# Attention and quantized feed-forward on one core: the values of a unit moved in front of the next scores, both in 64x64 tiles, with division and rotations moved to other places

## The chip, the cores and the metric

The kernel runs on one NeuronCore of a Trainium2 chip. The metric is the device time of one execution in microseconds (us); lower is better. A profile of one execution comes with it: it records every instruction of the engines and every transfer. The engines are TensorE (PE in the profile, with its weight loads as PEld), VectorE (DVE), ScalarE (ACT), GpSimd (POOL) and SyncE (SP), which here only starts transfers (DMAs).

## The reference

One transformer layer over 4 sequences of 512 tokens, 1024 channels, 16 heads of 64. Everything is float32 except the int8 weight of the second part.

```python
q = (x @ w_q.T).reshape(4, 512, 16, 64); k = ...; v = ...
q, k = rope(q), rope(k)                       # x * cos + rotate_every_two(x) * sin
scores = where(causal, einsum('bhqd,bhkd->bhqk', q, k), -1e9) / sqrt(64)
attn = softmax(scores, axis=-1)
out = einsum('bhqk,bhkd->bhqd', attn, v).reshape(4, 512, 1024)
x = layernorm(x + out @ w_out.T)
x = layernorm(x + x @ (weight * scales[:, None]).T)
```

## The kernel before

**Units.** A unit is one sequence and one pair of heads; there are 32 (`units`, L133), and the loop at L572 takes them one after the other. First come the units of sequences 0 and 1 in turn, then those of 2 and 3. While a unit `u` is in attention, TensorE also makes the q, k and v products of the units that follow: a product is 24 matmuls of 128x128 by 512 columns (`product`, L268: 16 of the parts h and l into one PSUM tile, 8 of the part d into another). These matmuls are dealt out as tickets by `take(n)`; a turn of the loop takes 72, in the order k of `u+1`, v of `u+1`, q of `u+2`. They fill the time in which TensorE would wait for the softmax.

**One turn of the loop** (L572 to L607): `scores(u)`: four blocks of 128 queries, in three groups (`GROUPS`, L121: blocks 0 and 1; block 2; block 3), each with its own PSUM tile; block `i` is multiplied with the keys of blocks 0 to `i`; the two heads sit in the two halves of the partitions, so a matmul has 64 rows and 128 columns of weights. `maxima` adds the causal mask to the diagonal block (VectorE, L427; for the three units in `BUSY` TensorE adds it, L419) and takes the maximum of each row (L430). `softmax` has ScalarE take the exponential with the sum of each row (L444), VectorE the reciprocal (L452) and GpSimd multiply the row by it (L458). `transposes` (L475) turns a group by 32x32 blocks on VectorE (L463), writes it to memory (`turned`, L464) and reads it back with keys on the partitions (`prT`, L472). `attend(u-1)` multiplies the transposed shares of the unit before with its values, 8 matmuls of 128 rows and 64 columns of weights, after 18 tickets (L490); ScalarE copies the result (L498) and starts its write to `ao` (L499).

**Other work in the turn.** At the 16th matmul of a product ScalarE takes the first sum out of PSUM into `tA` (L295), at the 24th VectorE joins the second sum to it (L318). For q and k, SP then starts two transfers that swap even and odd rows into `rot` (L249), and `rope` does two multiplications and an addition on VectorE (L235, L236, L242). The values are turned by `turn_values` (L463, L464, L482). After every second unit the weights change: `load_w` (L181) brings 512 KB for each of q, k, v into one of three stage buffers, ScalarE makes the part h and a scaled copy (L214, L215), VectorE the parts l and d (L219, L223). `later` and `run` put such steps into named slots of the turn.

**Order.** Between L502 and L608 TensorE, VectorE and ScalarE run in the order in which the program emits the work (`manual_schedule`). SP and GpSimd do not: the order of their instructions is left to the scheduler of the framework. After the loop come the output projection (L199), the first layer norm and the feed-forward part (L676).

Of the kernel before, what the change touches and what calls it, by code (L numbers as in the profile page):

```python
# [26 lines left out]
MASKED = -3.0e38  # L27
# [11 lines left out]
def attention_ffn_kernel(  # L39
# [29 lines left out]
    pdp = pds.enter_context(tc.tile_pool(name="pd", bufs=3, space=PSUM))  # L69

    ident = const.tile([P, P], FP, name="ident")
    mask, unit = (const.tile([P, P], BF, name=name) for name in ("mask", "unit"))
    cos_sb = const.tile([P, 2, S], FP, name="cos_sb")
    sin_sb = const.tile([P, 2, S], FP, name="sin_sb")
    eps_sb = const.tile([P, 1], FP, name="eps_sb")

# [3 lines left out]
    for n in (512, 384):  # L80
        nc.tensor.matmul(warm[:, :n], lhsT=sin_sb[:, 0, :P], rhs=sin_sb[:, 0, :n], start=True, stop=True)

    make_identity(nc, ident)
    make_identity(nc, unit)
    nc.gpsimd.memset(mask, 0.0)
    nc.gpsimd.affine_select(
        out=mask,
        in_=mask,
        pattern=[[-1, P]],
        compare_op=ALU.is_ge,  # L90
        fill=MASKED,
        base=0,
        channel_multiplier=1,
    )
    nc.gpsimd.memset(eps_sb, EPS)

# [31 lines left out]
    turned = {g: tc.dram_tile([R, P, w * 2 * Q], FP, name=f"turned_{g}") for g, w in enumerate(WIDE)}  # L128
    turned["v"] = tc.dram_tile([R, P, NI * Q], FP, name="turned_v")
# [99 lines left out]
    with tc.tile_pool(name="raw", bufs=2) as rawp, tc.tile_pool(name="qk", bufs=2) as qkp, ExitStack() as heads:  # L229
        def rope(u, k):  # L230

            raw, rot = prod.pop((u, k)), prod.pop(("rot", u, k))
            if u not in qk:
                qk[u] = qkp.tile([P, 2, S], FP, tag="qk", name=f"qk_{u}")
            nc.vector.tensor_mul(rot, rot, sin_sb[:, k, :])  # L235
            nc.vector.tensor_mul(raw, raw, cos_sb[:, k, :])  # L236
            out = qk[u][:, k, :]
            if k == 0:

                out = out.rearrange("p (i r s) -> p r i s", i=NI, r=R)  # L240
                raw, rot = (t.rearrange("p (r i s) -> p r i s", i=NI, r=R) for t in (raw, rot))
            nc.vector.tensor_add(out, raw, rot)  # L242

        def swap(u, k):

            raw = prod[u, k]
            rot = prod["rot", u, k] = rawp.tile([P, S], FP, tag="rot", name=f"rot_{u}_{k}", bufs=2)
            for p in range(2):
                nc.sync.dma_start(out=rot[p::2, :], in_=raw[1 - p :: 2, :])  # L249

        def raw_tile(u, k):
            tag = "v" if k == 2 else "raw"
            t = prod[u, k] = rawp.tile([P, S], FP, tag=tag, name=f"{tag}_{u}_{k}", bufs=1 if k == 2 else 2)
            return t
# [13 lines left out]
        def product(u, k, n):  # L268
# [24 lines left out]
            if n == 2 * NC - 1:  # L293
                prod["tA"] = rawp.tile([P, S], FP, tag="tA", name=f"tA_{u}_{k}")
                nc.scalar.activation(prod["tA"], ps, AF.Copy, scale=1.0 + X12)  # L295
                if x_next:
                    new_sequence(u, b_next, False)
                if more:
# [6 lines left out]
                    vector = ((u - 1, "first"), (u - 1, "late"), (u, "between"))[k]  # L305
                    if u == 1:
                        vector = (None, vector, (1, "between"))[k]
                    if last and k != 1:
# [5 lines left out]
                        later(*d, lambda: diff_w(k))  # L314
                    else:
                        later(*vector, lambda: split_w(k))
            if n == NT - 1:
                nc.vector.scalar_tensor_tensor(raw_tile(u, k), ps, -X12, prod["tA"], op0=MUL, op1=ADD)  # L318
                if k < 2:
                    swap(u, k)  # L320
                    slot = ("first" if last else "between" if u % 2 else "late") if k == 0 else "turn"
                    later(u - 1, slot, lambda: rope(u, k))
# [70 lines left out]
        probs, prT, stats, s_ps = {}, {}, {}, {}  # L393

        def scores(u):
            nmx = st1.tile([P, 2 * NI], FP, tag="nmx", name=f"nmx_{u}")
            den = st1.tile([P, 2 * NI], FP, tag="den", name=f"den_{u}")
            rden = st1.tile([P, 2 * NI], FP, tag="rden", name=f"rden_{u}")
            stats[u] = nmx, den, rden
            t = qk.pop(u)  # L400
            keys = t[:, 1, :].rearrange("p (r s) -> p r s", r=R)
            for g, blocks in enumerate(GROUPS):
                ps = pdp.tile([P, 2, 512], FP, tag="d", name=f"s_{u}_{g}")
                s_ps[u, g] = ps
                for i, at in blocks:
                    n = (i + 1) * P
                    for j in range(2):
                        rows = slice(j * D, (j + 1) * D)
                        nc.tensor.matmul(  # L409
                            ps[:, j, at : at + n],  # L410
                            lhsT=t[rows, 0, ts(i, P)],
                            rhs=keys[rows, :, : (i + 1) * Q],
                            start=True,
                            stop=u not in BUSY,
                        )
                    if u in BUSY:
                        diag = ps[:, :, at : at + n].rearrange("p a (r s) -> p a r s", r=R)[:, :, :, ts(i, Q)]
                        for j in range(2):
                            nc.tensor.matmul(diag[:, j], lhsT=unit, rhs=mask, start=False, stop=True)  # L419

        def maxima(u, g):
            nmx, den, rden = stats[u]
# [80 lines left out]
        with tc.manual_schedule(  # L503
# [68 lines left out]
            for u in range(NU):  # L572
                scores(u)
                run(u, "early")
                for g in range(3):
                    maxima(u, g)
# [195 lines left out]
```

## Time and profile before

| what | value |
|---|---|
| median of 3 runs | 1020.24 us (1019.99 to 1022.3) |
| span of the profiled execution | 1020.7 us |
| start up to the first scores | 33.4 us |
| the 32 units, from the first scores to the end of the last values | 33.4 to 738 us |
| output projection and feed-forward | 738 to 1020.7 us |
| TensorE busy between 381.1 and 681.3 us | 300.2 of 300.2 us |
| VectorE, ScalarE busy there | 257.0 us, 135.8 us |
| share of time the 16 DMA engines are busy there | 0.70 |
| one turn of the loop, in the plain stretches | 21.45 us |

In the profile an arrow reads "written from": `s<-qk` is the score tile made from the rotated q and k. A float32 matmul shows two records, one for each of two passes over its columns. An idle time before an instruction is put down to what ended it. Where the same turn of the loop is spoken of, its times are counted from a first matmul of that turn.

### The profile page before, as it was taken

The numbers are of one execution on the slowest core, as the hardware profiler recorded it, in microseconds if no ns is written. First come the engines' busy times: TensorE is split into PE (matmuls) and PEld (weight loads), VectorE is DVE, ScalarE is ACT, GpSimd is POOL, SyncE is SP. The second block draws the span as 40 slices with busy tenths as digits, with TensorE's granted clock in tenths as the row PEclk, the third lists the DMA queues.
The fourth block names the chain that finished last, engine by engine and source line by source line (L and its number), as shares of the span: only waits on it lengthen the run. The fifth ranks groups of instructions, "written<-read, shape, count | busy, mean of one in ns | idle before, by whom it ended". The sixth has DMA issues, their size and how long they took to land.

```text
span 1020.7 us, 13748 instructions
## 1 busy us (share of the span) xinstructions
PE 999.7 (98%) x4628; PEld 742.0 (73%) x4628; DVE 852.8 (84%) x1246; ACT 389.0 (38%) x841; POOL 201.1 (20%) x283
## 2 busy tenths in 40 slices
PE   9999999999999999999999999999899999999997
PEld 4667777777777667777777777776578888888885
DVE  5998888888888999788898888889877877878776
ACT  4534444354444435445344453445332122121110
POOL 0122332222322322332223322232100000000000
PEclk9999999999999999999999999999999999999999
DMA  7576676767768787576866758688635465564551
GB/s 288 170 233 220 203 234 190 263 195 223 232 193 261 250 254 227 183 253 192 253 210 206 247 173 273 217 250 278 223 108 160 124 160 143 128 168 104 145 103 62
DMA packets 264022, 204.09 MB, mean 200 GB/s; under 512 B 147600, under 2 KB 220304, under 8 KB 263824
## 3 DMA queue, kind: packets, MB, share of 16 engines
q1 hardware_dynamic: 256176, 184.60, 60.0%
q10 hardware_dynamic: 5616, 10.75, 2.9%
q0 software_dynamic: 2160, 7.87, 1.9%
q8 instruction: 37, 0.61, 0.3%
q14 instruction: 33, 0.27, 0.1%
HBM read 112.46 MB, written 73.92 MB: 183 GB/s over the span
## 4 chain that ended last, share of the span: by engine, by line
PE 85%; DMA 5%; issue 4%; DVE 4%; POOL 1%; SPq 0%; ACT 0%; DVEq 0%; POOLq 0%
PE p L276 43%; PE y L199 15%; PE f L676 11%; PE o L490 7%; PE s L409 6%; PE pw L261 2%; DMA turned<-pr 2%; DVE pr L463 1%; POOL pr L458 1%; DMA sx<-in_wo 1%; DMA prT<-turned 1%; DMA raw_x<-in_xT 1%; DVE w_l L219 1%; DMA va<-turned_v 0%; DMA turned_v<-v 0%
## 5 line engine op out<-in xcount | busy, mean ns | idle before, releaser
L458 POOL TENSOR_SCALAR pr<-pr,rden 128x128 f32<-128x128 f32 (+3 forms) x256 | 189.9, 760 | 525.9 <-DVE rden L452 414.5
L276 PE MATMUL p<-x_h,w_h 128*128 128x512 f32 x736 | 290.2, 394 | 0.0
L276 PE MATMUL p<-x_l,w_l 128*128 128x512 f32 x736 | 286.8, 390 | 0.0
L276 PE MATMUL p<-x_d,w_d 128*128 128x512 f32 x736 | 190.9, 395 | 3.1 <-DVE v L318 2.5
L276 PEld LDWEIGHTS p<-x_h,w_h 128*128 128x128 f32 x736 | 138.1, 188 | 50.3 <-issue 22.0
L444 ACT ACTIVATE pr<-s,nmx 128x128 f32<-128x128 f32 (+3 forms) x256 | 131.5, 531 | 112.6 <-DVE nmx L430 107.1
L276 PEld LDWEIGHTS p<-x_d,w_d 128*128 128x128 f32 x736 | 135.5, 188 | 36.4 <-issue 5.1
L276 PEld LDWEIGHTS p<-x_l,w_l 128*128 128x128 f32 x736 | 138.2, 188 | 28.1
L295 ACT ACTIVATE tA<-p 128x512 f32<-128x512 f32 x92 | 55.2, 600 | 218.4 <-PE p L276 218.4
L463 DVE STREAM_TRANSPOSE pr<-pr 128x768 f32<-128x768 f32 (+1 forms) x96 | 99.7, 1057 | 24.4 <-POOL pr L458 23.7
L430 DVE TENSOR_REDUCE nmx<-s 128x2 f32<-128x256 f32 (+3 forms) x128 | 101.9, 820 | 3.0
L199 PE MATMUL y<-x_l,w_l 128*128 128x512 f32 x256 | 100.1, 391 | 2.1 <-DVE w_l L219 2.1
L199 PE MATMUL y<-x_h,w_h 128*128 128x512 f32 x256 | 100.4, 392 | 0.5 <-DVE row L208 0.5
L676 PE MATMUL f<-wf,x1lo 128*128 128x512 f32 x240 | 93.6, 390 | 1.1 <-DVE x1lo L650 1.1
L676 PE MATMUL f<-wf,x1hi 128*128 128x512 f32 x240 | 93.5, 389 | 0.0
L409 PE MATMUL s<-qk 64*128 64x384 f32 (+3 forms) x512 | 80.2, 446 | 1.0 <-DVE qk L242 1.0
L490 PE MATMUL o<-prT,va 128*64 128x256 f32 (+3 forms) x512 | 77.7, 446 | 2.2 <-DMA prT<-turned 1.7
L223 DVE TENSOR_TENSOR w_d<-w_h,w_l 128x1024 fp32r<-128x1024 f32 x60 | 74.0, 1233 | 1.5
L318 DVE SCALAR_TENSOR_TENSOR raw<-p,tA 128x512 f32<-128x512 f32 x61 | 41.8, 686 | 37.1 <-PE p L276 37.0
L490 PEld LDWEIGHTS o<-prT,va 128*64 128x64 f32 x512 | 34.8, 138 | 48.6 <-issue 42.6
L199 PE MATMUL y<-x_d,w_d 128*128 128x512 f32 x256 | 64.9, 393 | 1.6 <-DVE x_d L177 1.2
L409 PEld LDWEIGHTS s<-qk 64*128 64x128 f32 x512 | 41.4, 186 | 22.4 <-issue 11.3
(112 smaller groups left out, 1162.1 us busy)
## 6 DMA issues: line engine op xcount, KB each, us to landing
turned<-pr SPq DMA_DIRECT2D x64, 384.0 KB, 3.4
rot<-raw SPq DMA_DIRECT2D x128, 128.0 KB, 2.8
turned<-pr SPq DMA_DIRECT2D x32, 512.0 KB, 4.5
prT<-turned SPq DMA_DIRECT2D x32, 512.0 KB, 5.2
prT<-turned SPq DMA_DIRECT2D x32, 384.0 KB, 3.9
turned_v<-v SPq DMA_DIRECT2D x32, 256.0 KB, 5.0
va<-turned_v SPq DMA_DIRECT2D x128, 64.0 KB, 2.6
prT<-turned SPq DMA_DIRECT2D x32, 256.0 KB, 3.3
```

Of the source, the lines that this page charges most:

```text
L199: nc.tensor.matmul(ps, lhsT=r[part][:, c, :], rhs=w[part][:, c, :], start=n in (0, 2 * NC), stop=n in (2 * NC - 1, NT - 1),)
L223: nc.vector.tensor_tensor(d, h, l, SUB)
L276: nc.tensor.matmul(ps, lhsT=w[part][:, c, :], rhs=r[part][:, c, :], start=n in (0, 2 * NC), stop=n in (2 * NC - 1, NT - 1),)
L295: nc.scalar.activation(prod["tA"], ps, AF.Copy, scale=1.0 + X12)
L318: nc.vector.scalar_tensor_tensor(raw_tile(u, k), ps, -X12, prod["tA"], op0=MUL, op1=ADD)
L409: nc.tensor.matmul(ps[:, j, at : at + n], lhsT=t[rows, 0, ts(i, P)], rhs=keys[rows, :, : (i + 1) * Q], start=True, stop=u not in BUSY,)
L430: nc.vector.tensor_reduce(nmx[:, 2 * i : 2 * i + 2], ps[:, :, at : at + n], AX.X, ALU.max, negate=True)
L444: nc.scalar.activation(pr[:, :, at // P : at // P + i + 1, j, :], ps[:, j, at : at + n].rearrange("p (r k s) -> p r k s", r=R, s=Q), AF.Ex ...
L458: nc.gpsimd.tensor_scalar(p, p, rden[:, m : m + 1], 1.0, ALU.mult, ALU.mult)
L463: nc.vector.transpose(t, t)
L490: nc.tensor.matmul(ps[j * D : (j + 1) * D, kb * P :], lhsT=v[:, kb, 2 * j : 2 * j + 2, :].rearrange("p a s -> p (a s)"), rhs=t[:, :, 4 * k ...
L676: nc.tensor.matmul(ps, lhsT=part[:, c, :], rhs=wfv[:, c, o], start=(c == 0 and part is hi), stop=(c == NC - 1 and part is lo),)
```

## The change

Part by part:

1. **Place and tiling of the matmuls.** `attend(u-1)` stands right in front of `scores(u)`. Both work in tiles of 64 rows by 64 columns of weights. The halves of odd blocks are swapped in the order of tokens (`by_row`), and keys that lie after all queries of a half block are left out. The values of the upper and the lower 64 keys of a block go to two PSUM banks; ScalarE copies one and VectorE the other, GpSimd adds them. The PSUM tile of the values is now that of score group 0 (`ps_d[0]`).
2. **Division.** The shares are no longer divided (no L458). The sums of the rows are inverted, turned, written to memory and fetched again spread over the partitions (`shares`, `fetch_shares`), and GpSimd multiplies the values by them (`attended`).
3. **Rotations** of all units but the first run on GpSimd.
4. **Order.** Largest block first: groups 2, 1, 0. The reading back of the turned shares (`fetch`) stands apart from the writing and after the next 8 tickets. GpSimd and SP now also run in the order of the program, and the write to `ao` is started by SP.
5. The masks are built otherwise, with 32 small transfers at the start; `tA` is gone (the first sum goes straight into the raw tile); raw tiles have one buffer each; some slots of `later` are others.

```diff
-    pdp = pds.enter_context(tc.tile_pool(name="pd", bufs=3, space=PSUM))
+    pdp = pds.enter_context(tc.tile_pool(name="pd", bufs=1, space=PSUM))
+    ps_d = [pdp.tile([P, 2, 512], FP, name=f"s_{g}") for g in range(3)]
...
+        def rope(u, k, engine=nc.gpsimd):
+            pair = prod.pop((u, k))
+            raw, rot = pair[:, 0, :], pair[:, 1, :]
...
-            nc.vector.tensor_mul(rot, rot, sin_sb[:, k, :])
-            nc.vector.tensor_mul(raw, raw, cos_sb[:, k, :])
-            nc.vector.tensor_add(out, raw, rot)
+            engine.tensor_tensor(rot, rot, sin_sb[:, k, :], MUL)
+            engine.tensor_tensor(raw, raw, cos_sb[:, k, :], MUL)
+            engine.tensor_tensor(qk[u][:, k, :], raw, rot, ADD)
...
-                    vector = ((u - 1, "first"), (u - 1, "late"), (u, "between"))[k]
+                    vector = ((u - 1, "first"), (u - 1, "late"), (u - 1, "last"))[k]
...
+                    elif k < 2:
+                        later(*vector, lambda: split_w(k))
                     else:
-                        later(*vector, lambda: split_w(k))
+                        later(*vector, lambda: low_w(k))
+                        later(u, "then", lambda: diff_w(k))
...
-                    slot = ("first" if last else "between" if u % 2 else "late") if k == 0 else "turn"
-                    later(u - 1, slot, lambda: rope(u, k))
+                    later(u - 1, "turned_q" if k == 0 else "turned_k", lambda: rope(u, k))
...
@@ scores @@
+            for g in (2, 1, 0):
+                blocks = GROUPS[g]
+                ps = s_ps[u, g] = ps_d[g]
                 for i, at in blocks:
+                    for c in range(2):
+                        early = i * P + c * D
+                        if i % 2 != c:
+                            pieces = ((0, (i + 1) * P),)
+                        elif c == 0:
+                            pieces = ((0, early + D),)
+                        else:
+                            pieces = ((0, i * P), (early, early + D))
+                        for j in range(2):
+                            rows = slice(j * D, (j + 1) * D)
+                            for s0, s1 in pieces:
+                                nc.tensor.matmul(
+                                    ps[c * D : (c + 1) * D, j, at + s0 : at + s1],
+                                    lhsT=t[rows, 0, early : early + D],
+                                    rhs=t[rows, 1, s0:s1],
...
@@ softmax @@
-                    nc.gpsimd.tensor_scalar(p, p, rden[:, m : m + 1], 1.0, ALU.mult, ALU.mult)
...
+        def shares(u):
+            nmx, den = stats.pop(u)
+            nc.vector.reciprocal(rden[:, : 2 * NI], den)
+            t = st1.tile([P, Q], FP, tag="rdenT", name=f"rdenT_{u}")
+            nc.vector.transpose(t, rden)
+            nc.sync.dma_start(out=turned["d"].rearrange("a c s -> (a c) s"), in_=t)
+
+        def fetch_shares(u):
+            share[u] = otp.tile([P, R, P], FP, tag="share", name=f"share_{u}")
+            for j in range(2):
+                nc.sync.dma_start(
+                    out=share[u][j * D : (j + 1) * D],
+                    in_=turned["d"][:, j * NI : (j + 1) * NI, :].rearrange("a c s -> a (c s)").partition_broadcast(D),
+                )
...
@@ attend @@
+            for kb in range(NI):
+                for h in range(2):
+                    for j in range(2):
+                        rows = slice(h * D, (h + 1) * D)
...
+                        if h == kb % 2:
+                            piece(kb * P, later_blocks(kb))
+                        else:
+                            c = 1 - kb % 2
+                            piece(kb * P + c * D, t[rows, 2 * c : 2 * c + 2, 4 * kb, j, :])
+                            if kb < NI - 1:
+                                piece((kb + 1) * P, later_blocks(kb + 1))
+            nc.scalar.copy(o[0], ps[:, 0, :])
+            nc.vector.tensor_copy(o[1][:, D:], ps[:, 1, D:])
+
+        def attended(u):
+            nc.gpsimd.tensor_tensor(o[:, D:], o[:, D:], o1[:, D:], ADD)
+            o_by = o.rearrange("p (i a s) -> p i a s", i=NI, s=Q)
+            nc.gpsimd.tensor_tensor(o_by, o_by, share.pop(u).rearrange("p a (i s) -> p i a s", s=Q), MUL)
+            nc.sync.dma_start(out=ao[b][:, hp, :], in_=o)
...
@@ the turn of the loop @@
+                if u:
+                    attend(u - 1)
                 scores(u)
                 run(u, "early")
+                for g in (2, 1):
+                    maxima(u, g)
+                    softmax(u, g)
+                fetch_values(u)
+                if u:
+                    attended(u - 1)
+                run(u, "turned_q")
+                take(18)
+                transposes(u, 2)
+                maxima(u, 0)
+                softmax(u, 0)
+                transposes(u, 1)
+                transposes(u, 0)
                 run(u, "between")
                 run(u, "then")
+                take(8)
+                shares(u)
+                for g in (2, 1, 0):
+                    fetch(u, g)
+                fetch_shares(u)
                 run(u, "after")
                 run(u, "first")
                 run(u, "turn")
                 run(u, "mid")
+                take(10)
                 run(u, "second")
                 take(12)
+                run(u, "turned_k")
                 run(u, "late")
                 take(12)
                 if u + 1 < NU:
                     turn_values(u + 1)
+                run(u, "last")
                 take(12)
                 run(u, "end")
```

## The prediction

> **What bounds the kernel now.** I read the page's busy shares first, then the chain of waits in order of time, then single engines over one turn of the loop, then the transfers.
>
> ```profile
> PE 999.7 (98%) x4628; PEld 742.0 (73%) x4628; DVE 852.8 (84%) x1246; ACT 389.0 (38%) x841; POOL 201.1 (20%) x283
> ...
> 466.92 2.36 PE s L409 x16
> 469.28 4.32 PE p L276 x18
> 473.60 2.31 PE o L490 x16
> 475.91 12.46 PE p L276 x54
> 488.37 2.36 PE s L409 x16
> ...
> L409 PE MATMUL s<-qk 64*128 64x512 f32 x128 | 33.1, 594 | 0.0
> L261 PE MATMUL pw<-raw_x,raw_w 128*128 128x512 f32 x48 | 21.7, 606 | 0.3 <-DMA raw_x<-in_xT 0.3
> ...
> 482.82 0.60 SPq L181 DMA_DIRECT2D sw<-in_wq  x1
> 508.54 1.05 ACT L214 ACTIVATE w_h<-sw 128x1024 fp32r<-128x1024 f32 x1
> 524.63 0.58 SPq L181 DMA_DIRECT2D sw<-in_wq  x1
> 527.25 1.84 SPq L472 DMA_DIRECT2D prT<-turned  x2
> ...
> 466.85:509.75 42.90, 42.90 (x210) 31.44 (x209) 36.47 (x54) 19.28 (x47) 11.60 (x16) 1.00 0.70 221
> ...
> prT<-turned SPq DMA_DIRECT2D x32, 512.0 KB, 5.2
> ao<-ot ACTq DMA_DIRECT2D x32, 256.0 KB, 2.1
> sw<-in_wq SPq DMA_DIRECT2D x14, 512.0 KB, 5.7
> ```
>
> The chain is TensorE alone: scores, 18 tickets, values, 54 tickets, 21.45 us a turn, with no wait. Only what shortens TensorE's own work can gain, and only while everything else still arrives in time. The last lines tell how it arrives now: weights for q are loaded at 482.82 and first used at 508.54, 25.7 us later, because the scheduler places SP's instructions freely; the DMA engines are busy 0.70 of the time.
>
> **The matmuls.** Tickets start 0.227 us apart (477.33, 477.56, 477.78 in TensorE's timeline), so 72 take 16.34, and 21.45 - 16.34 = 5.11 us a turn go to scores, values and the changes between shapes. A 512-column pass of one full-array float32 matmul takes 21.7/48 = 0.45 us. The four records of 512 columns in a unit's scores keep TensorE busy 33.1/32 = 1.03 us with tail, two passes of 0.43: the two heads run at once, and in the timeline their records start in pairs. So a column costs 2 x 0.84 ns, 1280 columns take 2.15 us in scores and as much in values, and 5.11 - 4.30 = 0.81 us is lost at four changes of shape. After it, counted from the code, each of the four tiles has 1152 columns in scores and 1152 in values: 2 x 1.94 = 3.88. Two changes of shape are left: 0.40. A turn of TensorE's work is 16.34 + 3.88 + 0.40 = 20.62, **0.83 less; over 32 units -26 us**. No row shows four tiles at once. The one end is this; the other is that a matmul can't start before the one ahead of it in the program. As pieces for one tile follow each other directly, I count 1600 and 1408 columns then: 5.05 us, 1.17 more, and the turn is 21.8 instead of 20.62 (+0.35 against now). I take the first, by the nearest row: the program gives the first head's matmul with both passes before the second head's, yet the records of the two heads start within 0.01 us of each other and the next two 0.2 to 0.4 us later. So a pass that waits for its tile does not hold up the other tile.
>
> The Trainium skill speaks against that: "TensorE: Matmul & The Clock Gate", Part 3 (row/col tiling), says that matmuls start and end strictly in program order. By the page the turn would be 21.8, by the row 20.62.
>
> **What else moves.** VectorE loses six rotation operations (L235, L236, L242: 0.69 to 0.71 us each, 4.2 a turn) and gets a copy (0.6, like L318's 0.69), a reciprocal (0.17, L452) and a small transpose (under 0.7, L463's 128x512). It isn't on TensorE's path, so the gain is cover only. GpSimd loses 8 multiplications (5.5 to 6.1 us a turn in its timeline) and gets 8 two-input ones over 448 or 512 columns. None is in the trace: the bounds are its own one-input row (L458, 128x512, 0.71) and twice that; I take 1.1, between, 9 us of 20.6. The k rotation starts when its swap lands, 16 us into the turn, and is due at the next scores, 22.6: hidden up to 2.2 us an operation, beyond both bounds.
>
> The skill's "GPSIMD Engine Reference", section 4.1, advises against two-input elementwise work there, at about half VectorE's pace. By the 4497 ns that its section 3.1 gives for 2048 columns an operation would be 1.1 us (an estimate), still hidden.
>
> The masks at the start (32 small transfers) are due at the first scores, 33 us in: hidden by the loads and the first products; without that cover a late mask would cost its delay once. The last unit's wait for its shares (1.7 among the waits) can go: 0 to -2. At the change of sequences, from 334.0 to 381.1, TensorE is busy 43.97 of 47.10 us, so 3.1 us are lost now; SP will take the loads of x in program order there: nothing to as much again, I take +2.
>
> **Two new waits**, timed in an odd turn, zero at the first matmul of the values. Values end at 2.0, the first two groups of scores at 3.4, all at 4.0; the 24th ticket ends at 9.6, the 64th at 18.7, the turn at 20.6.
> VectorE: copy to 2.8; mask and maxima of block 3 to 4.7 (0.46 + 1.14 apart in its timeline), block 2 to 6.0; transpose of group 2, after ScalarE's exponentials (1.33 a pair), 6.1 to 7.2; masks and maxima of blocks 0 and 1 to 9.1; group 1 to 10.1; group 0, after exponentials to 10.2, to 11.2; w_d of v (L223, 1.2) to 12.4; L318 to 13.0; sums to 13.4.
> SP, in program order: three writes (7.2, 10.1, 11.2), the swap of k (two at 0.55, from 13.0), the sums' write, then the four reads of `prT` from 14.5, the sums' reads to 16.9, and only then the weights of q.
> DMA: a turn moves 4608 KB (turned 1280, `prT` 1280, swaps 512, turned values 256 and 256, `ao` 256, weights 768 on average) in 0.70 x 21.45 = 15.0 us, 3.3 us per 1024 KB. An uncrowded one, `ao`, needs 2.1 us, so about 1.3 beyond its 0.8 of bytes.
>
> *Shares.* Bytes of `prT` begin some 0.8 (of the 1.3) after the first read, at 15.3, behind the swap, last 4.2 to 19.5, and land at 20.0, or at 21.8 if the crowd costs 1.8 of the 2.2 by which the row of 512 KB (5.2) lies above 1.7 + 1.3. Due at 20.6. Even turns lack w_d, but the late weights below push their start. **+0.7 a turn (0 to 1.2), 30 turns, +21 us.** Behind this wait stand the scores and all tickets.
>
> *Weights.* After the shares' 4.2 and the sums' 256 KB (0.8) the bytes of the weights of q run from 20.3 to 22.0 and land at 22.5, or 23.7 in a crowd (the row of that very load has 5.7 in all, 16.9 + 5.7 = 22.6). ScalarE has their split (L214, L215: 1.06 + 1.06) in its order ahead of the copy of the values (0.59): 25.3 to 26.5. The third group of scores reuses the values' PSUM tile and is due at 20.6 + 0.7 + 3.4 = 24.7, so TensorE stands 0.6 to 1.8 us; behind the copy on ScalarE are the next unit's exponentials. **I take the middle, 1.2, in 14 turns (x14 in the DMA row): +17 us.**
>
> Sum on the profile's 1020.7: -26 + 21 + 17 + 2 = +14, **1035 us**. The median of the runs, 1020.24, is 0.5 lower: no correction.
>
> **Rivals.**
> *Faster: the transfers land in time.* The place is the queue behind SP, the condition that `prT` lands by 20.6 and the weights by 21.2 (24.0 less 2.8), 1.3 us before the early end of my line. Then TensorE alone sets the turn: 1020.7 - 26 = 995. For it: VectorE is freed of 4 us, large blocks go first. Against: SP's fixed order, and 5.7 us for the load now.
> *Half and half.* Only one of the two waits is real: 1020.7 - 26 + 17 or + 21, with the 2: 1014 or 1018; I say 1015, as the weights' is the surer.
> *The tiles don't overlap as counted.* Strict order of starts: 32 x 0.35 = +11 in place of -26. Against the forecast the due times move out by 1.2 and the start of the softmax by 0.5, so each wait shrinks by 0.7: 0 x 30 + 0.5 x 14 = 7, or with the crowded ends 0.5 x 30 + 1.1 x 14 = 30. With the 2 that is 1041 to 1064; I say 1052.
>
> **How the numbers follow.** Forecast (two waits, 1023 to 1052) 0.48; in time, 995: 0.20; half, 1015 (1006 to 1023): 0.14; strict order, 1052: 0.18. The range 1002 to 1058 leaves out most of the second and the top of the last, 0.19 together. Under 0.3% (1017.2 to 1023.3) a measurement can't tell it from no change. Faster: 0.20 + 0.06 = 0.26; same: 0.06 + 0.02 = 0.08; slower: 0.66. The forecast's own range is 1023 to 1052.
>
> **What would show it.** Right: in every second turn TensorE waits before scores of 64x64 tiles, on ScalarE's copy, which follows w_h, which waits for sw; and before the values on `prT`; values and scores together take about 3.9 us. Wrong: TensorE without gaps and turns of 20.6; or values and scores over 4.6 us, which is the order of starts; or weights issued early; or waits on the rotations of GpSimd.

## The result, and the profile after it

The changed kernel takes **1193.62 us** (median, 1189.62 to 1200.37) against 1020.12 us for the kernel before on the same chip: ratio **1.171, 95% interval 1.166 to 1.175**. It is 17% slower; 1035 us were predicted, and the range ended at 1058. Its profiled execution has a span of 1195.2 us.

The first view is the page of the changed kernel: busy times, and the span in 40 slices with the granted clock.

```profile
PE 1041.9 (87%) x6292; PEld 817.2 (68%) x6292; DVE 778.2 (65%) x1060; ACT 390.6 (33%) x841; POOL 369.3 (31%) x314
...
PE   6988988889888778889988898987859999999997
...
PEclk8899999899999889999999898999979999999999
```

TensorE was busy 98% of the span and is now at 87%; no other engine is above 65%. So no engine has become the bound: the time is in waits. The first 30 slices carry them, which are the units. Two stages of each kernel, the units and what follows, with their length in front of the comma and the granted clock in the third column from the end, first after, then before:

```profile
44.86:911.70 866.84, 735.29 (x5017) 578.72 (x5016) 538.36 (x700) 320.72 (x746) 336.33 (x248) 0.94 0.64 196
911.70:1195.20 283.50, 272.72 (x1210) 224.62 (x1208) 220.57 (x342) 55.76 (x80) 13.15 (x20) 0.99 0.50 128
```

```profile
33.38:737.90 704.52, 693.91 (x3345) 503.10 (x3346) 612.50 (x887) 317.90 (x747) 189.94 (x256) 1.00 0.72 227
737.90:1020.70 282.80, 274.15 (x1218) 225.45 (x1214) 217.61 (x338) 56.05 (x80) 9.64 (x16) 0.99 0.48 127
```

The units take 866.8 us instead of 704.5, and they begin at 44.9 us instead of 33.4. What comes behind them is unchanged (283.5 us here, 282.8 before). A turn of the loop, from one first matmul of the values to the next, is 25.88 us in the twelve turns from 499.16 to 809.72 us; it was 21.45.

Who waits on TensorE (engine, line, what released it: us in total, times, longest):

```profile
PE s L533 <- DMA prT<-turned: 42.1, 14, 6.9
PE s L533 <- DMA share<-turned_d: 26.0, 11, 3.6
PE s L425 <- DVE ot L555: 23.8, 13, 3.3
```

L533 are the values, L425 the scores. Both waits that the prediction named are there, at the places that it named. The label of the second line needs care: the shares are not an input of TensorE. In the turn shown below the last read of `prT` landed at 524.32 us, 0.35 us ahead of the values, and the first of the shares only at 524.84, when the values were already running. So lines one and two are one wait, for `prT`.

One turn shows the chain of the late weights (start, duration, engine; in brackets idle time before and its releaser):

```profile
516.95 2.18 SPq L506 DMA_DIRECT2D prT<-turned  x4
519.18 2.04 SPq L486 DMA_DIRECT2D share<-turned_d  x2
521.27 0.60 SPq L193 DMA_DIRECT2D sw<-in_wq  x1
...
524.67 2.22 PE L533 MATMUL s<-prT,va 64*64 64x512 f32 x41 [2.04 <-DMA share<-turned_d]
526.65 0.59 PE L425 MATMUL s<-qk 64*64 64x512 f32 x1
526.68 0.27 PE L533 MATMUL s<-prT,va 64*64 64x128 f32 x1
...
527.18 1.06 ACT L226 ACTIVATE w_h<-sw 128x1024 fp32r<-128x1024 f32 x1 [5.67 <-DMA sw<-in_wq]
...
529.23 0.57 ACT L554 COPY ot<-s 128x512 f32<-128x512 f32 x1
529.83 0.62 DVE L555 COPY ot<-s 128x448 f32<-128x448 f32 x1 [6.41 <-ACT ot L554]
...
530.51 0.88 PE L425 MATMUL s<-qk 64*64 64x64 f32 x20 [2.04 <-DVE ot L555]
```

SyncE issues the weights of q only behind the reads of `prT` and of the shares. ScalarE waits 5.67 us for them. Its copy of the values stands behind that split, and **VectorE's copy waits for ScalarE's** (6.41 us), although it reads the other half of the tile. The prediction didn't have that last wait: VectorE's masks and maxima, with which the next chain begins, stand behind it too. In the other direction one line is worth a look: a score (L425) starts at 526.65, ahead of the last values (L533) at 526.68. TensorE's four tiles run at once and overtake each other.

### The profile page after: what moved, and what is told of

Same layout as the page of the kernel before. It is cut to its first block, busy times and chain, and to the rows that moved or that the text cites. A ratio compares the mean times of both kernels' runs of the same rounds, so it can differ in the third digit from the quotient of the medians.

```text
span 1195.2 us, 17113 instructions
## 1 busy us (share of the span) xinstructions
PE 1041.9 (87%) x6292; PEld 817.2 (68%) x6292; DVE 778.2 (65%) x1060; ACT 390.6 (33%) x841; POOL 369.3 (31%) x314
## 5 line engine op out<-in xcount | busy, mean ns | idle before, releaser
L284 PE MATMUL p<-x_d,w_d 128*128 128x512 f32 x736 | 184.1, 392 | 11.5 <-DVE raw L329 10.1
L533 PE MATMUL s<-prT,va 64*64 64x64 f32 (+4 forms) x1408 | 105.4, 435 | 82.5 <-DMA prT<-turned 42.1
L284 PEld LDWEIGHTS p<-x_d,w_d 128*128 128x128 f32 x736 | 136.8, 188 | 46.5 <-DVE raw L329 16.5
L466 ACT ACTIVATE pr<-s,nmx 128x512 f32<-128x512 f32 (+3 forms) x256 | 131.5, 526 | 107.4 <-DVE nmx L452 69.0
L248 POOL TENSOR_TENSOR raw<-raw,sin_sb 128x512 f32<-128x512 f32 x62 | 82.2, 1326 | 256.3 <-DMA raw<-raw 256.3
L533 PEld LDWEIGHTS s<-prT,va 64*64 64x64 f32 x1408 | 76.4, 166 | 115.3 <-issue 94.2
L329 DVE SCALAR_TENSOR_TENSOR raw<-p,raw 128x512 f32<-128x512 f32 x92 | 62.4, 679 | 82.6 <-PE p L284 80.9
L425 PE MATMUL s<-qk 64*64 64x64 f32 (+5 forms) x1280 | 93.9, 390 | 23.8 <-DVE ot L555 23.8
L452 DVE TENSOR_REDUCE nmx<-s 128x2 f32<-128x1024 f32 (+3 forms) x128 | 102.1, 820 | 3.0
L302 ACT ACTIVATE raw<-p 128x512 f32<-128x512 f32 x92 | 54.7, 594 | 144.3 <-PE p L284 116.4
L425 PEld LDWEIGHTS s<-qk 64*64 64x64 f32 x1280 | 73.1, 147 | 40.6 <-DVE ot L555 36.2
L250 POOL TENSOR_TENSOR qk<-raw 128x512 f32<-128x512 f32 x62 | 92.7, 1496 | 4.9
```

The lines of the kernel that those rows point to most:

```text
L248: engine.tensor_tensor(rot, rot, sin_sb[:, k, :], MUL)
L250: engine.tensor_tensor(qk[u][:, k, :], raw, rot, ADD)
L284: nc.tensor.matmul(ps, lhsT=w[part][:, c, :], rhs=r[part][:, c, :], start=n in (0, 2 * NC), stop=n in (2 * NC - 1, NT - 1),)
L302: nc.scalar.activation(raw_tile(u, k), ps, AF.Copy, scale=1.0 + X12)
L329: nc.vector.scalar_tensor_tensor(r, ps, -X12, r, op0=MUL, op1=ADD)
L425: nc.tensor.matmul(ps[c * D : (c + 1) * D, j, at + s0 : at + s1], lhsT=t[rows, 0, early : early + D], rhs=t[rows, 1, s0:s1], start=s0 == 0 ...
```

## The experiments

My theory: the chain scores, maxima, exps, turn, write, read of `prT`, values has become the length of a turn, drawn out by SyncE's fixed order and by the clock. Rivals: the four 64x64 tiles are dear in themselves; GpSimd's rotations set the turn; the start explains it. All times are medians of four runs, ratios against the kernel before on the same chip. In runs whose edits add lines, line numbers are shifted.

**The values moved back** (from in front of the scores to behind 36 tickets).

```
-                if u:
-                    attend(u - 1)
                 scores(u)
...
                 take(8)
                 shares(u)
+                take(10)
+                if u:
+                    attend(u - 1)
+                    attended(u - 1)
                 for g in (2, 1, 0):
                     fetch(u, g)
```

> The only edit: a unit's values leave the place in front of the next scores and go behind 36 tickets of the product stream, as far from the reads of prT as in the kernel before; tiles, division, rotations and block order stay as changed. Theory (a chain scores, maxima, exps, turn, write, read, values has become the length of a turn, drawn out by waits and by the low clock after each of them): the chain is cut, TensorE bounds again at about 16.3 us of product stream + 4.3 of values and scores + 0.4 = 21.0 us a turn, the units fall from 866.9 to 680-705 us, the whole to 1010-1035 us. Rival one (the four 64x64 tiles are the slower matmuls): their number and place on TensorE's own queue cost the same, above 1150 us. Rival two (GpSimd's slow rotations): they are untouched, so above 1120 us.

Measured: 1219.54 us, ratio 1.195 (1.191 to 1.200). **My expectation failed.** TensorE never waits for `prT` here, yet turns of some 31 and of 21.4 to 24 us, from scores to scores, alternate. The reason stands in a long one:

```profile
368.79 0.61 SPq L193 DMA_DIRECT2D sw<-in_wq  x1
...
374.52 1.06 ACT L226 ACTIVATE w_h<-sw 128x1024 fp32r<-128x1024 f32 x1 [8.00 <-DMA sw<-in_wq]
...
379.67 0.50 PE L284 MATMUL p<-x_h,w_h 128*128 128x512 f32 x1 [4.13 <-ACT raw L302]
```

The weights of q are as late as before, and what now stands behind the split on ScalarE are the exps and the copies that free the product's accumulators, so TensorE stops in the product stream (59.3 us in 29 waits for that copy). The late load costs its time wherever the values are. A second wait shows here too: the scores stand 52.7 us, in 19 waits, for GpSimd's last step of the k rotation. The changed kernel has no such wait.

**Rotations on VectorE** (`engine=nc.gpsimd` to `engine=nc.vector` in `rope`).

> The only edit: the rotations of all units go back to VectorE, in the same places of the order. Theory (chain through the values, late weights, clock): VectorE gets six operations of about 0.6 us a turn, three of them ahead of its turn of the largest block, so the chain gets longer rather than shorter: 1190-1260 us. Rival two (GpSimd's rotations set the turn): the rotations end earlier, the time falls to 1130 us or less. Rival three (only the start and its mask transfers matter): no change, 1188-1200 us.

Measured: 1245.68 us, ratio 1.220 (1.217 to 1.222). GpSimd's rotations are not what makes the changed kernel slow; on VectorE they make it slower.

**Weights ahead.**

```
+        def ahead(u):
+            return u % 2 == 1 and 3 <= u < NU - 1 and u != 15
...
-            if more and n == 0:
+            if more and n == 0 and not ahead(u):
                 load_ao(k) if last else load_w(k, units[u + 1][1])
...
+                if ahead(u + 2):
+                    load_w(0, units[u + 3][1])
+                if ahead(u + 1):
+                    load_w(1, units[u + 2][1])
+                    load_w(2, units[u + 2][1])
                 fetch_values(u)
```

> The only edit: SyncE issues the loads of the next pair's weights a turn's start ahead (W_q before the reads of the values in the odd turn, W_k and W_v in the even turn) instead of behind the reads of prT. Theory: the split of W_q on ScalarE no longer waits for its load, the copies of the values go on time in the 14 turns that follow such a load, and 2 to 3.8 us of TensorE's wait for group 0 with the low clock after it goes there: 14 x (2.5 to 4.5) = 35 to 63 us less, 1130-1160 us. Rivals (tiles, rotations, start): no change, 1186-1200 us.

Measured: **1130.79 us**, ratio 1.108 (1.104 to 1.111): 62.8 us less, and ordinary turns of 23.2 us. The wait of the scores for the copy is gone but for one of 3.1 us. The edit moves the loads for k and v as well as that for q; no run separates them.

**Order of the two copies** (VectorE's written first).

> The only edit: of the two copies of the values' result, VectorE's is written ahead of ScalarE's. Theory: VectorE's copy no longer waits for ScalarE's (31 waits, 166.7 us in all in the changed kernel), so VectorE's maxima of the two large groups go on time also where ScalarE stands in front of a late W_q. ScalarE's exps and TensorE's group 0 still wait behind the late split, so only a part comes back: 1160-1190 us. If the two copies were not held apart by a wait of one on the other, no change: 1188-1200 us.

Measured: 1164.96 us, ratio 1.143 (1.138 to 1.148), 28.7 us less. Now ScalarE's copy waits for VectorE's, 108.3 us in 19 waits: whichever is written second waits for the first.

**Both together, weights ahead and copy order.**

> Two edits together: weights loaded ahead, and VectorE's copy in front of ScalarE's. Alone they gave 1130.8 and 1165.0 us against 1193.6, 63 and 29 us. Theory: both take away the same stall (ScalarE standing before W_q, VectorE behind ScalarE), so they do not add: 1115-1131 us. If they were separate costs they would add: 1100 us.

Measured: 1123.45 us, ratio 1.101 (1.098 to 1.105). As expected the gains don't add; the order of the copies is worth 7.3 us once the weights are in time.

**The masks' buffer apart.**

```
-    with tc.tile_pool(name="mask", bufs=2) as maskp:
+    by_token = const.tile([P, 2, P], BF, name="by_token")
+    with ExitStack():
...
-            by_token = maskp.tile([P, 2, P], BF, tag="by_token", name="by_token")
```

> The only edit: the tile in which the masks are built lies in a buffer of its own, kept to the end, instead of a pool that is closed and whose memory the stage of the loads takes over; both masks are built in it one after the other. Theory: SyncE's load of the second sequence (first one at 23.88 us in the changed kernel, behind the last mask transfer) starts at about 7.5 us, the first scores move from 44.9 to 33-36 us, and nothing else changes: 1182-1187 us. Rival three (the start explains the loss): 1030 us or less.

Measured: 1178.64 us, ratio 1.155 (1.152 to 1.159), 15.0 us less, somewhat more than expected; 11.1 us of it lie at the start: the first scores start at 33.7 us instead of 44.9, nearly as before the change (33.4). In the changed kernel the start reads so:

```profile
15.02 7.64 POOL L104 DMA_DIRECT2D bounds<-by_token  x16
23.88 0.33 SPq L177 DMA_DIRECT2D sx<-in_xT  x1
...
27.81 1.06 ACT L181 ACTIVATE x_h<-sx 128x1024 fp32r<-128x1024 f32 x1 [12.67 <-DMA sx<-in_xT]
```

The masks themselves aren't needed early. But the pool in which they are built is closed, the next pool takes its memory, and so SyncE's load of the second sequence waits until the last mask transfer is done, with all that follows on SyncE.

**Values back and weights ahead; then also GpSimd's finishing of the values behind the k rotation.**

```
                     attend(u - 1)
-                    attended(u - 1)
                 for g in (2, 1, 0):
                     fetch(u, g)
-                fetch_shares(u)
...
                 run(u, "turned_k")
+                if u:
+                    attended(u - 1)
+                fetch_shares(u)
```

> Two edits together: the values go back behind 36 tickets, and the weights are loaded a turn's start ahead. In the run with the values moved back alone, turns of 31.3 and 21.4 to 24 us alternated, and the long ones are those in which ScalarE's split waits for W_q in front of the exps. Theory: with the late load gone the long turns fall to about 22 us, 14 x 9 = 126 us less than that run's 1219.5: 1060-1100 us; what is left above 21.0 us a turn is GpSimd's queue, where the k rotation stands behind the finishing of the values. Rival one (the four 64x64 tiles are slower matmuls): still above 1150 us.

> As the run before it, and on GpSimd the finishing of the values goes behind the k rotation (with the reads of the shares behind it on SyncE). Theory: no wait is left in the turn, TensorE bounds it with 16.3 + 4.3 + 0.4 = 21.0 us: the units take 680-705 us, the whole 1005-1035 us, no slower than 1.5% above the kernel before although the start still costs its 11.5 us. Rival one (tiles) and rival two (GpSimd's rotations as such): 1100 us or more.

Measured: 1139.54 us, ratio 1.117 (1.114 to 1.119), and 1109.28 us, ratio 1.087 (1.085 to 1.090). Both stayed above what I expected. In the second the shortest turns are 21.3 us, so the tiles are not dear, but the others take 21.7 to 24.4 us from scores to scores, and TensorE waits there for GpSimd's last step of the k rotation (27.7 us, 22 times) and for ScalarE's copies in the product stream (12.3 us, 18 times). So rival two is not the cause in the changed kernel, but stands right behind it.

**There the k rotation on VectorE, and the masks apart** (`rope(u, k, nc.vector if k else nc.gpsimd)`).

> Values back, weights ahead and GpSimd's order as in the run of 1109.3 us; in addition the k rotation alone goes to VectorE and the masks' buffer is kept apart. There TensorE waited for GpSimd's last step of the k rotation 22 times, 27.7 us in all. Theory: with the chain cut GpSimd's rotation of k is the next limit; on VectorE it takes 2.1 us instead of 4.6, the waits go: 25-35 us less, and 12-15 us less at the start: 1060-1075 us, ordinary turns of 21.3 us. Rival (VectorE becomes the limit): ordinary turns longer than 22.3 us, 1090 us or more.

Measured: **1059.15 us**, ratio 1.038 (1.037 to 1.040); ordinary turns of 21.87 and 22.17 us. With the values back this is the best that was found, and it is slower than the kernel before.

**Reads of `prT` ahead** (on top of weights ahead, values in front).

```
                 transposes(u, 0)
+                for g in (2, 1, 0):
+                    fetch(u, g)
...
                 shares(u)
-                for g in (2, 1, 0):
-                    fetch(u, g)
                 fetch_shares(u)
```

> Weights ahead as before (1130.8 us alone), and SyncE issues the reads of prT right behind the last write of the turned exps, in front of the swap of k and the write of the shares, where they stood behind both. In an ordinary turn of the run with weights ahead prT's reads are issued 16.3 to 18.4 us behind the values' start and TensorE stands 1.5 to 2.3 us in front of the next values. Theory (the chain through prT is the length of the turn): the last read goes out about 2.5 us sooner, the wait falls to the 0.3 us of a change of shape, an ordinary turn from 23.0 to 21.4-21.8 us: 24 turns x 1.4 = 34 us and some at the sequence change: 1080-1102 us. Rival (TensorE waits there for something else, GpSimd's rotation of k or the shares): these come later than before, 1125 us or more.

Measured: 1114.28 us, ratio 1.092 (1.090 to 1.094): 16.5 us less, about half of the expectation. TensorE hardly waits for `prT` any more (1.0 us in all; the values start 0.32 us behind the last ticket in 28 of 32 turns, as in the kernel before), and a new wait has come between values and scores:

```profile
PE s L428 <- POOL qk L250: 38.7, 31, 2.3
```

The swap of k now stands behind the reads of `prT` on SyncE, and the rotation of k is late in its place.

**All four together** (weights, copy order, reads, masks).

> All that was found and that leaves the values in front of the next scores: weights ahead, VectorE's copy first, prT's reads ahead, masks apart. Theory: 1130.8 less 7 (copy order) less 28-50 (prT's reads) less 12-15 (start) = 1060-1085 us; the two changes of sequence and the last units keep their waits of some 45 us, so it stays slower than the kernel before. Rival (the four tiles cost by themselves): ordinary turns stay above 22.3 us.

Measured: 1104.29 us, ratio 1.083 (1.079 to 1.087), 19 us above the expected range, and ordinary turns of 22.7: the same wait, 37.1 us. Turns above 22.3 were the sign of the rival, but 1.1 us of an ordinary turn is this wait, so they don't speak for dear tiles. One turn of it:

```profile
457.71 1.29 POOL L248 TENSOR_TENSOR raw<-raw,sin_sb 128x512 f32<-128x512 f32 x1 [12.47 <-DMA raw<-raw]
...
460.31 1.26 POOL L250 TENSOR_TENSOR qk<-raw 128x512 f32<-128x512 f32 x1
...
461.63 2.24 PE L428 MATMUL s<-qk 64*64 64x512 f32 x40 [0.69 <-POOL qk L250]
```

GpSimd has stood idle 12.47 us for the swap before it begins. Is it its pace, then, or the swap's place?

**The k rotation on VectorE, and then the loads of the next sequence ahead too.**

> The kernel with all four repairs and the values in front of the scores (1104.3 us), and the k rotation alone on VectorE. There TensorE no longer waits for prT at all (0.32 us ahead of the values in 28 turns) but stands 0.8 to 2.4 us between values and scores, 31 times, 37.1 us in all, for the last GpSimd step of the k rotation. Theory (GpSimd's rotation is the third chain, which comes to light once the other two are shorter): the waits go, ordinary turns fall from 22.7 to 21.4-21.9 us, the whole to 1064-1078 us. Rival (VectorE, standing for the swap of k, is late with its own work): no gain, 1095 us or more.

> As the run before it, and the first three loads of the next sequence's input (and of the output weights behind the last sequence) are issued at the start of the turn ahead instead of behind the swap of k in front of prT's reads. Theory: at the two changes of sequence ScalarE's splits no longer stand for these loads in front of the copies of the values; of the 5 to 7 us above an ordinary turn that turns at the change take, 3 to 5 go in each of two turns: 6-12 us less than the run before. Rival (the change is dear through the splits' own work on ScalarE and VectorE): within 3 us of the run before.

Measured: 1140.45 us, ratio 1.117 (1.115 to 1.120), and 1139.71 us, ratio 1.115 (1.113 to 1.118). **The rival was right**: VectorE itself stands 130.2 us for the swap of k (32 times), and its copies, splits and maxima behind it. The second of the two tells nothing, as this loss covers its place.

**The swap of k from ScalarE's queue** (rotation back on GpSimd), **and then the loads of the next sequence ahead.**

```
-                    swap(u, k)
+                    swap(u, k, nc.scalar if k else nc.sync)
...
+                if u + 1 in (14, 30):
+                    for n in range(3):
+                        load_x2(2 if u + 1 == 14 else B, n)
```

> The kernel with all four repairs and the values in front of the scores (1104.3 us); the only further edit: the swap of k goes out from ScalarE's queue, where it follows the product's update at once, and no longer behind prT's reads on SyncE (in the odd turns 3.3 us behind that update). GpSimd keeps the rotation. Theory (the third wait comes from SyncE's order, which can have either prT or the swap in time, not from GpSimd's pace): GpSimd begins 2 to 3 us sooner, the 37.1 us of waits between values and scores go, ordinary turns 21.3-21.9 us, 1064-1080 us. Rival (GpSimd's pace, three steps of 1.3 us and two for the values): at most a third goes, 1090 us or more.

> As the run before it, and the first three loads of the next sequence at the start of the turn ahead (units 14 and 30). Theory: ScalarE no longer stands in front of its split until they land (8.2 us at the first change), the turns of 28.9 and 27.2 us there lose 3 to 6 us in all and those in front of the last unit as much: 6-12 us less than the run before. Rival (the splits' own work): within 3 us of it.

Measured: 1094.58 us, ratio 1.071 (1.069 to 1.074), and **1084.45 us**, ratio 1.063 (1.060 to 1.065). Between 440 and 700 us both waits are gone, 0.2 us is left of the one for the rotation, and turns alternate between 21.7 and 22.6. So the third wait was SyncE's order: with one queue either `prT` or the swap of k comes too late. The time of the first of the two, though, is one that the rival allowed for (1090 us or more): it gained 9.7 us instead of 24 to 40, because a fourth wait took the place:

```profile
466.11 1.14 ACTq L256 DMA_DIRECT2D raw<-raw  x2
467.30 1.06 ACT L226 ACTIVATE w_h<-sw 128x1024 fp32r<-128x1024 f32 x1 [2.80 <-DMA turned<-pr]
...
469.99 0.50 PE L287 MATMUL p<-x_h,w_h 128*128 128x512 f32 x1 [1.40 <-ACT raw L305]
```

ScalarE can start the swap only when VectorE's update of k is done (at 466.08), and until 467.30 it does nothing else; its next split begins 14.6 us into the turn (12.3 in the same turn of the run before), its copy of the next product's first sum (L305) comes late, and TensorE stops in the product stream. In the 25 ordinary turns the wait for the rotation fell from 28.5 to 0.7 us, and the wait for that copy rose from nothing to 17.2. The loads of the next sequence ahead gain another 10.1 us, at the change of sequences and in the last turns.

**The clock.** Ten matmuls that compute nothing needed, in front of the values; then five, and none where they would stand for an operand that is being rewritten.

```
                 if u:
+                    for n in range(10):
+                        nc.tensor.matmul(
+                            ps_d[2][:, 0, :], lhsT=WD[1][0][:, 0, :], rhs=X1[0][:, 0, :], start=True, stop=True
+                        )
                     attend(u - 1)
```

> The changed kernel with ten matmuls of 128x512 that compute nothing needed (about 2.3 us at full clock) in TensorE's order right in front of the values, where it stands waiting for prT; no wait is taken away. Theory (idle of about 3 us is followed by 3.41 us at half the clock, 28 such windows and 60 us lost in the units of the changed kernel): TensorE does not stand for long there, most windows go, and the time falls by 15-40 us to 1155-1180 us. Rival (the clock is no part of it): the added matmuls fill idle time at best, 1190-1215 us.

> The changed kernel with five added matmuls (1.1 us) in front of the values, none at the two places where the ten of the first such run stood for an operand being rewritten (12.1 us there). The shortest wait in front of the values in the changed kernel is 1.4 us, so five fit into every one and delay nothing, while the idle time left falls by 1.1 us a turn. Theory (the low clock behind long waits lengthens the chain): windows at half clock fall from 28 to 12-20, and with them the time, by 8-25 us, to 1168-1186 us. Rival (the half-speed stretches lie where TensorE would wait anyway, the chain does not run through them): windows fall as much and the time stays, 1189-1199 us.

Measured: 1199.32 us, ratio 1.175 (1.173 to 1.178), and 1197.87 us, ratio 1.174 (1.170 to 1.178). The granted clock rose, the time didn't fall:

```profile
core 0: 1195.8 us, clock 0.973
```

That is the first of the two; the changed kernel had 0.946 in a span of 1195.2. The trace's rows of half clock from the first scores on add up to 60 us lost in the changed kernel, 29 with ten and 48 with five added matmuls. **Neither run bears out my theory of the clock**: it goes along with the waits, and no run shows it as a cause of the time. Nor is it excluded as a small one: the ten matmuls last longer than many of the waits that they fill (1.0 to 3.6 us in ordinary turns) and stood 12.1 us for an operand at two places, so they may have lost again what the clock gave, and the five took only 12 of the 60 us away. With the weights ahead, where ordinary turns lose next to nothing to the clock (3.4 us in 24 turns), TensorE still waits for `prT` in each of them, so that wait doesn't need a low clock.

## Why the prediction was wrong

The direction, both waits and their places were right. Every size on the losing side was too small, and two costs were taken as none: the masks, and VectorE's wait for ScalarE's copy. The term that was furthest off is *Weights*, 1.2 us a turn counted and 4.5 measured. The terms, against the 173.5 us that were measured:

| term | predicted | measured |
|---|---|---|
| TensorE's own turn | -26 | -13 |
| ordinary turns above that, weights in time (*Shares*) | +21 | +54, of it 38 in front of the values |
| late weights (*Weights*) | +17 | +63 |
| masks at the start | 0 | +15 |
| change of sequences, last units | +2 | the rest, about 55 |

How the right column is made (its lines come from different runs and need not add up exactly): the shortest turn that any run shows with the values in front is 21.03 us, from 232.54 to 253.57 us with the k rotation on VectorE, with no wait of TensorE in it; 21.03 - 21.45 = -0.42, times 32. With the weights ahead 25 ordinary turns take 23.2 us in the mean, 2.2 above that: 54. TensorE's idle time in front of the values is 38 us of it; some 7 us are waits in the product stream. The third and fourth are differences of medians, 1193.6 - 1130.8 and 1193.6 - 1178.6. The rest is what is left; in the trace of the run with the weights ahead 44 of it can be seen: 6.4 us in the first turn, 15.3 at the change of sequences, 22.6 in the last three turns, each against the same work before.

*The tiles.* The step was right in kind: four tiles do run at once, 44 records of the values start within 2.12 us (1.94 predicted) and the 40 of the scores within 2.34. From the first of the values to the first ticket behind the scores it takes 4.49 us where 3.88 + 0.40 were counted. The strict order of starts, 5.05 us for the matmuls alone, is excluded, also by the score that starts ahead of the last values; the rule that the prediction quotes against its row doesn't hold here. Half of the gain was still not there.

*Shares: the step that failed is "copy to 2.8".* The prediction let the two copies of the values run at the same time. The trace with the weights in time shows them one behind the other:

```profile
463.56 2.23 PE L536 MATMUL s<-prT,va 64*64 64x512 f32 x41 [1.21 <-DMA prT<-turned]
...
465.99 0.58 ACT L557 COPY ot<-s 128x512 f32<-128x512 f32 x1 [4.76 <-PE s L536]
...
466.60 0.62 DVE L558 COPY ot<-s 128x448 f32<-128x448 f32 x1 [1.91 <-ACT ot L557]
...
477.98 1.14 SPq L256 DMA_DIRECT2D raw<-raw  x2
...
479.85 2.05 SPq L509 DMA_DIRECT2D prT<-turned  x4
```

From the first values at 463.56: VectorE's copy ends at 3.66 (2.8 predicted), the first write goes out at 8.1 (7.2), the swap of k at 14.4 (13.0), the reads of `prT` at 16.3 (14.5), and the next values begin at 23.6. Half of the 1.8 us is the copy. From the first read to the next values it takes 7.3 us, the late end of what was allowed for (14.5 to 21.8). So TensorE stands 1.5 us a turn in front of the values instead of 0.7, outside the range of 0 to 1.2, and the turn is 2.2 us above 21.03. The same step is in the next term: in the changed kernel the order of the two copies alone was worth 28.7 us, with the weights in time 7.3.

*Weights: the mechanism was right, its reach was not.* Predicted was one wait of 1.2 us in 14 turns. In the turn from 499.16 us the load went out at 22.1 (16.9 predicted) and ScalarE's copy came at 30.1 (25.3 to 26.5), because each step ahead of it was already late. And more stood behind it than one group of scores: VectorE by way of the copy, and so the softmax of the next turn, whose `prT` is late again. Moving the loads gave 62.8 us, 4.5 for each of the 14.

*Masks.* "Hidden by the loads" named the wrong user of the cover. The masks were in time; the loads waited for them, through the memory that both use in turn.

*GpSimd* was costed at nothing, and rightly so in the changed kernel, where TensorE never waits for it. The three steps of its rotations took 1.33, 1.45 and 1.50 us in the mean (1.1 taken, bounds 0.71 to 1.42, so two lie outside). But the cover was the wait for `prT`: when that was taken away, the k rotation cost 38.7 us, by way of its swap.

*Change of sequences, last units.* The +2 stood for three loads in SyncE's program order. These loads go out ahead of the reads of `prT`, and ScalarE's splits stand for them in front of the copy: the same two waits again, longer.

None of the rivals came true. All of them, like the forecast, priced each wait once, as if the next turn began on time.

What stays open: the 64 us by which the best version with the values in front is above the kernel before were not followed by an experiment. Ordinary turns (22.2 against 21.45 us) make about 20 of them, as much as TensorE's waits for ScalarE's copies and VectorE's updates in the product stream (21.6 us in the 25 turns); the trace puts the others at the first turn, the change of sequences and the last units. Copies that don't wait for each other were not tried, and how much of the time the low clock costs was not settled. No version found beats the kernel before.

## What to carry to other kernels

A chain that is moved next to its consumer has a slack of one turn less its own length, and everything that shares a queue with it comes out of that slack. Work it out with the late end of each transfer and with each pair of engines that touch one tile taken in turn; if little or nothing is left, price the wait in every turn, and again in what it makes late. When a queue's order is written by hand, look first at what the scheduler had been placing early, here the weights, a turn ahead of their use. And a buffer that is closed is not gone: whoever gets its memory waits for its last reader.

## What was not expected of the hardware

**GpSimd and VectorE hold each other up** when both work on two operands in SBUF. In the run with the swap of k on ScalarE's queue:

```profile
460.10 1.30 POOL L248 TENSOR_TENSOR raw<-raw,sin_sb 128x512 f32<-128x512 f32 x1 [1.17 <-DMA raw<-raw]
...
467.58 1.23 DVE L235 TENSOR_TENSOR w_d<-w_h,w_l 128x1024 fp32r<-128x1024 f32 x1
...
471.82 2.21 DVE L235 TENSOR_TENSOR w_d<-w_h,w_l 128x1024 fp32r<-128x1024 f32 x1
...
472.91 2.27 POOL L249 TENSOR_TENSOR raw<-raw,cos_sb 128x512 f32<-128x512 f32 x1
```

Where they don't meet, the two take 1.30 and 1.23 us; overlapping, 2.27 and 2.21. Beside VectorE's other operations, those that read PSUM above all, GpSimd stays at 1.3 us (111 steps in this run, none above 1.32). The Trainium skill has this in "SBUF — State Buffer", section "SBUF: two separate sides": VectorE with two inputs in SBUF and GpSimd take one pair of ports in turn, whole instructions at a time. The trace agrees, and the prediction, which moved six such operations a turn to GpSimd, should have used it.

**The clock** falls to half for 3.41 us, or a multiple of it, behind waits of TensorE: 28 such stretches in the changed kernel, two before. In all 26 of them that lie in the units TensorE was busy for less than half of the 3.41 us ahead. The Trainium skill, "TensorE: Matmul & The Clock Gate", Part 1, warns of idle time of more than about 3.4 us. In these rows less is enough: the wait of 2.04 us that ends at 530.51, shown above, is followed by half the clock from 531.16 us. The two fills cut the time that was lost so from 60 to 29 and 48 us without a gain.
